# Gated cross-attention and a quantised FFN on one core: where the next tokens are normalised, and who orders VectorE

## The chip, the cores and the metric

The kernel runs on one core of one Trainium2 chip. The metric is the device time of one execution in microseconds. A core has five engines that run side by side, each with its own queue in which instructions start in order: TensorE (PE in the profile; its weight loads are shown apart as PEld), VectorE (DVE), ScalarE (ACT), GpSimd (POOL) and SyncE (SP), which here only issues DMAs. They wait for each other by semaphores.

## The reference

The shapes are x (8, 256, 1024), the context (8, 256, 1024), square attention weights of 1024, and FFN weights of 2752 x 1024 (gate, up) and 1024 x 2752 (down), all f32. Cut to what matters:

```python
def fake_quant(t, axis):                       # symmetric, 127 steps
    s = maximum(max(abs(t), axis) / 127, 1e-8)
    return clip(round(t / s), -128, 127) * s

def xattn(text, f):
    Q = text @ Wq.T + bq;  K = f @ Wk.T + bk
    return softmax(Q @ K.T / sqrt(1024)) @ f   # values are the raw context

def ffn(x):
    gate, up = qlinear(x, w_gate), qlinear(x, w_up)   # inputs and weights fake-quantised by row
    return qlinear(silu(gate) * up, w_down)

x = x + tanh(g_xattn) * xattn(layernorm(x), ctx)
x = x + tanh(g_ffn) * ffn(layernorm(x))
```

## The kernel before

**Tiles.** There are B = 8 sequences of 256 tokens; a sequence is NTT = 2 tiles of 128 tokens. The width 1024 is KC = 8 chunks of 128, or two halves of 512. The FFN width 2752 is 21 chunks of 128 and one of 64, which the code handles as NPR = 11 pairs.

**First stage, to about 108 us.** The product of the two attention weights is formed once (seven half-size products, L313), so that scores are tokens times this matrix `mt` times context.

**Attention loop (L645 to L695), b = 0 to 6, about 46 us each.** The scores of sequence b are formed in `softmax_stage`, which also transposes the already normalised tokens `xn` of b+1 on TensorE; ScalarE copies the transposes into `xT` (L436). Then the queries H of b+1 are formed in eight parts (`queries_between(0)` to `(7)`, L508, copied out by ScalarE at L512). Between these parts lie the rest of the work of sequence b and the preparation for later ones: two calls of `attend` (the "attended halves" are the two token tiles of b), `residual` (VectorE, L566), the statistics of the new tokens x2 (`Rows.sums`, `root`, `inverse`), their normalising and rounding steps (`steps`, `store_steps`), storing x2 to HBM through GpSimd's queue (L667, L674), transposing the context of b+1 (`features_transposed`), and loading and normalising the tokens xn of b+2 (L661 and L680 to L691). `prepare()` is a software pipeline over the FFN weights: SyncE loads a piece, VectorE takes its row maxima (L118) and the inverse of the step, GpSimd scales it (L209, L221), ScalarE rounds it (L245, L234), and it is transposed or stored by DMA. A piece passes these three steps in three successive calls.

From L164 to L928 `tc.manual_schedule()` holds: every engine runs its instructions in the order in which the code writes them.

**The last attention with the first FFN block (L882 to L928), about 469 to 516 us.** The pairs of the FFN's first block lie between the parts of the last sequence's attention.

**FFN (L941 to L1009).** A block is one sequence. `gate_up(block, p)` forms pair p: `products` fills a bank g and a bank tr (L749, two of each), VectorE multiplies gate by the token's step (`silu_gate`, L758), ScalarE applies Silu (L760), VectorE makes h (`hidden`, L773), ScalarE takes its absolute value (L779), and `fold` keeps a running maximum (L790). A block's down products (`down_pair`, L854) fill four banks (tags s and a) with the rounded hidden tiles `hq` of the block before; between its eleven pairs the maxima of the newer block become steps (`block_max`, `block_scales`), are spread over the partitions through two ScalarE instructions and two transposes (`broadcast_rows`, L712, L713) and are copied out as `ib` (L826), and `quantised` makes the next hq: VectorE's product (L839) and a rounding by VectorE (L841) or by two ScalarE instructions (L843, L844). `down_end` takes each of the four outputs (two token tiles, two halves) out of its bank (VectorE, L871), adds the residual xr (GpSimd, L874) and stores it (L875); `o` has three buffers, xr two.

In this part only TensorE has its order from the code:

```python
order.enter_context(tc.manual_schedule(engines={mybir.EngineType.PE}))
```

The order on VectorE, ScalarE, GpSimd and SyncE comes from a planner, which places instructions by its own estimate of when they can run.

Of the kernel before, what the change touches and what calls it, by code (L numbers as in the profile page):

```python
# [17 lines left out]
P = 128  # L18
# [9 lines left out]
def gated_xattn_ffn_kernel(  # L28
# [26 lines left out]
    nc = tc.nc  # L55
    B, S, D = x.shape
# [109 lines left out]
    if True:  # L166
# [347 lines left out]
        def features_transposed(b, g, copy):  # L514
            quarter_transposed(fT, [f_tiles[b][:, l, :] for l in range(NLT)], g, copy)

        def load_tokens(b, tag):
            tiles = []
            for t in range(NTT):
                tiles.append(work.tile([P, D], F32, name=tag, tag=tag))  # L520
                nc.sync.dma_start(out=tiles[t], in_=x[b, t * P : (t + 1) * P, :])
            return tiles
# [22 lines left out]
        def numerators_transposed(pe):  # L545
            pt = transposes(pe, range(NLT))
            pT = work.tile([P, NLT, P], F32, name="pT", tag="pT", bufs=1)
            nc.scalar.copy(pT, pt[:, :NLT, :])
            return pT
# [93 lines left out]

        waiting = None
        for b in range(B - 1):  # L645
            nums = softmax_stage(b, xn)
            tokens_bias(b + 1, xn, scratch)
            if waiting:
                store_steps(*waiting)
            queries_between(0)  # L650
            xr = load_tokens(b, "xr")
            pT = numerators_transposed(nums[0][0])
            prepare()
            queries_between(1)
            pas = attend(b, pT)
            pT = numerators_transposed(nums[1][0])
            residual(b * NTT, pas, xr[0], nums[0][1])
            prepare()
            queries_between(2)
            if b + 2 < B:  # L660
                xn = load_tokens(b + 2, "xn")  # L661
            features_transposed(b + 1, 0, nc.scalar.copy)
            pas = attend(b, pT)
            residual(b * NTT + 1, pas, xr[1], nums[1][1])
            stats = Rows()
            stats.sums(0, xr[0])
            nc.gpsimd.dma_start(out=x2_dram[b * NTT], in_=xr[0])  # L667
            prepare()
            queries_between(3)
            stats.sums(1, xr[1])  # L670
            stats.root()
            if b + 2 < B:
                load_features(b + 2, (f_right, f_left)[b % 2])
            nc.gpsimd.dma_start(out=x2_dram[b * NTT + 1], in_=xr[1])  # L674
            features_transposed(b + 1, 1, nc.scalar.copy)
            stats.inverse()
            queries_between(4)
            y = steps(b * NTT, xr[0], stats)
            features_transposed(b + 1, 2, nc.scalar.copy)
            if b + 2 < B:  # L680
                stats_n = Rows()
                for t in range(NTT):
                    stats_n.sums(t, xn[t])
            queries_between(5)
            store_steps(b * NTT, y)
            features_transposed(b + 1, 3, nc.scalar.copy)
            if b + 2 < B:
                stats_n.root()
                stats_n.inverse()
                for t in range(NTT):  # L690
                    normalise(xn[t], xn[t], stats_n, t)  # L691
            queries_between(6)
            y = steps(b * NTT + 1, xr[1], stats)
            queries_between(7)
            waiting = (b * NTT + 1, y)  # L695
# [242 lines left out]

    order.enter_context(tc.manual_schedule(engines={mybir.EngineType.PE}))  # L941
    ALL = [(t, half) for t in range(NTT) for half in range(NH)]
    for p in range(9, NPR):
        gate_up(first, p)
# [18 lines left out]
    for b in range(1, B):  # L963
        if b > 1:
            block = {"xq": xq, "sx": sx_next, "h": []}
            for p in range(NPR):
                gate_up(block, p)
        if b + 1 < B:
            xq, sx_next = load_quantised(b + 1), sx
        pds = down_start()  # L970
        next_hq = []
        for p in range(NPR):
            down_pair(pds, hq, p, ALL)
            if p == 3:
                am = block_max(block, "g")
            if p == 5:
                next_sh, ib = block_scales(b, am, "tr")
            if p == 7 and b + 2 < B:
                sx = token_steps(b + 2, "g")
            if p > 4:  # L980
                for q in range(len(next_hq), NPR if p == NPR - 1 else len(next_hq) + 2):
                    next_hq.append(quantised(block["h"][q], ib, q))
            if b == 1 and p in (1, 2, 3, 4):
                n = 2 * P
                pb = bank("tr")
                broadcast_rows(pb[:, :n], swd[:, 2 * p - 2 : 2 * p], late[0])
                nc.scalar.copy(swd_bc[:, (p - 1) * n : p * n], pb[:, :n])
        down_end(b - 1, pds, sh, ALL)
        sh, hq = next_sh, next_hq

    pds = {key: bank(tag) for key, tag in zip(ALL, ("g", "tr", "s"))}
    for key in ALL[:3]:
        for p in range(NPR):
# [50 lines left out]
```

## Time and profile before

| | |
|---|---|
| runs shown, us | 951.08, 953.9, 5640.63; median 953.9 |
| the profiled execution's own time, us | 949.75 |
| its span, first to last instruction, us | 948.0 |
| TensorE busy, us | 930.9 |
| VectorE busy, us | 640.3 |
| ScalarE busy, us | 370.0 |
| GpSimd busy, us | 151.6 |

All lines come from that one execution. A row of the order of time gives start and duration in us, engine, line, operation, out<-in with shapes, a count, and in brackets how long the engine had been idle before it and what ended that. A row of the list of waits gives who waited for whom, the sum in us, how often, and the longest. A row of the groups gives count, busy us and mean ns of one. "PE ps_g L508" is TensorE writing a bank of tag g at line 508. The parts of the attention loop begin with the first query product of a sequence, at 146.54, 192.89, 239.65, 287.87, 335.29 and 381.37 us.

### The profile page before, as it was taken

To read this page: it belongs to the slowest core of one execution; us is meant where nothing else is said; L and a number is where in the kernel's file an instruction comes from. 1 tells how busy PE (TensorE), PEld (TensorE's weight loads), DVE (VectorE), ACT (ScalarE), POOL (GpSimd) and SP (SyncE) were. 2 spreads that over 40 slices of the span, in tenths; PEclk is the share of its full clock that TensorE was granted. 3 is DMA by queue.
4 is the path that set the end of the run, shared out by engine and by line. 5 is a ranking of instruction groups with operands and counts; after the bars stand their busy time and mean duration, and the time that the engine had idled before them with its cause. 6 is when DMAs were issued, how large, how long until landed. Compare 5 with 4: busy or idle time off the path is not lost.

```text
span 948.0 us, 14269 instructions
## 1 busy us (share of the span) xinstructions
PE 930.9 (98%) x5496; PEld 692.2 (73%) x5496; DVE 640.3 (68%) x1326; ACT 370.0 (39%) x668; POOL 151.6 (16%) x160
## 2 busy tenths in 40 slices
PE   9999999999999999999999999999999999999997
PEld 5444687878687878787878867858678685876854
DVE  5976834959585868686467857675676666667673
ACT  0122434545454535454547862414324143341410
POOL 0032311121221221221100003011030110303005
PEclk9999999999999999999999999999999999999999
DMA  9256776959597887978393712012121111201004
GB/s 345 99 148 226 211 213 183 335 184 301 191 265 251 238 257 234 235 252 236 103 191 74 148 23 90 9 30 76 23 90 23 31 59 23 90 1 67 25 1 156
DMA packets 125716, 135.95 MB, mean 143 GB/s; under 512 B 90256, under 2 KB 91536, under 8 KB 125648
## 3 DMA queue, kind: packets, MB, share of 16 engines
q1 hardware_dynamic: 112368, 104.36, 40.3%
q0 software_dynamic: 4784, 16.52, 4.4%
q10 hardware_dynamic: 8496, 14.16, 4.1%
q8 instruction: 43, 0.70, 0.3%
q14 instruction: 25, 0.20, 0.1%
HBM read 87.04 MB, written 26.74 MB: 120 GB/s over the span
## 4 chain that ended last, share of the span: by engine, by line
PE 61%; DVE 17%; issue 9%; DMA 6%; ACT 4%; POOL 2%; SPq 1%; ACTq 0%; DVEq 0%; POOLq 0%
PE ps_tr L749 10%; PE ps_g L749 10%; PE ps_g L508 10%; PE ps_s L508 5%; PE ps_a L555 4%; PE ps_a L854 4%; PE ps_s L854 4%; PE ps_s L313 4%; PE ps_a L313 4%; DVE h L839 3%; PE ps_s L526 2%; PE ps_g L313 2%; DMA out_dram<-o 2%; DMA wdq_dram<-rq 2%; PE ps_tr L413 2%
## 5 line engine op out<-in xcount | busy, mean ns | idle before, releaser
L508 PE MATMUL ps_g<-xT,mt 128*128 128x256 f32 x640 | 145.2, 380 | 3.7 <-ACT xT L436 3.7
L508 PEld LDWEIGHTS ps_g<-xT,mt 128*128 128x128 f32 x640 | 119.9, 190 | 24.3 <-ACT xT L436 5.9
L760 ACT ACTIVATE g<-g,swg 128x256 f32<-128x256 f32 (+1 forms) x176 | 79.7, 500 | 147.2 <-DVE g L758 146.6
L854 PEld LDWEIGHTS <-hq 128*128 128x128 bf16 x726 | 71.1, 98 | 74.7
L773 DVE SCALAR_TENSOR_TENSOR h<-ps_tr,swu,g 128x256 f32<-128x256 f32 x168 | 74.7, 482 | 48.5 <-ACT g L760 45.1
L209 POOL TENSOR_SCALAR raw<-raw,inv 128x1024 f32<-128x1024 f32 (+1 forms) x44 | 54.6, 1242 | 256.3 <-DVE inv L114 148.4
L874 POOL TENSOR_TENSOR o<-o,xr 128x512 f32<-128x512 f32 x31 | 39.7, 1281 | 327.8 <-DVE o L871 239.4
L749 PE MATMUL ps_tr<-xqb,wuT_lo 128*128 128x256 bf16 x704 | 84.7, 273 | 2.6 <-DVE h L773 2.6
L508 PE MATMUL ps_s<-xT,mt 128*128 128x256 f32 x384 | 86.9, 379 | 0.0
L790 DVE TENSOR_TENSOR acc<-acc,g 128x512 f32<-128x512 f32 (+2 forms) x88 | 56.4, 642 | 42.0 <-ACT g L779 41.2
L749 PE MATMUL ps_g<-xqb,wgT_lo 128*128 128x256 bf16 x704 | 84.7, 273 | 0.0
L749 PE MATMUL ps_tr<-xqb,wuT_hi 128*128 128x256 bf16 x640 | 77.7, 273 | 0.2
L749 PE MATMUL ps_g<-xqb,wgT_hi 128*128 128x256 bf16 x640 | 77.7, 273 | 0.2 <-DVE g L758 0.2
L245 ACT ACTIVATE rq<-raw,nmagic 128x1024 bf16<-128x1024 f32 (+1 forms) x44 | 50.6, 1149 | 69.4 <-POOL raw L209 60.3
L508 PEld LDWEIGHTS ps_s<-xT,mt 128*128 128x128 f32 x384 | 71.2, 190 | 8.7
L749 PEld LDWEIGHTS <-wuT_lo 128*128 128x128 bf16 x704 | 68.9, 98 | 11.5 <-issue 3.6
L749 PEld LDWEIGHTS <-wgT_lo 128*128 128x128 bf16 x704 | 69.0, 98 | 9.7 <-issue 0.6
L839 DVE TENSOR_TENSOR h<-h,ib 128x512 f32<-128x512 f32 x88 | 57.0, 683 | 22.1 <-ACT ib L826 22.1
L749 PEld LDWEIGHTS <-wuT_hi 128*128 128x128 bf16 x640 | 62.6, 98 | 7.9 <-issue 0.6
L749 PEld LDWEIGHTS <-wgT_hi 128*128 128x128 bf16 x640 | 62.6, 98 | 7.6 <-issue 0.4
L779 ACT ACTIVATE g<-h 128x512 f32<-128x512 f32 (+2 forms) x88 | 51.8, 590 | 38.5 <-DVE h L773 37.7
L566 DVE SCALAR_TENSOR_TENSOR xr<-ps_a,r,xr 128x512 f32<-128x512 f32 x32 | 23.9, 751 | 62.3 <-PE ps_a L555 62.2
(177 smaller groups left out, 1375.6 us busy)
## 6 DMA issues: line engine op xcount, KB each, us to landing
raw<-in_L_ffn_w_down_dram SPq DMA_DIRECT2D x32, 512.0 KB, 6.1
raw<-in_L_ffn_w_gate_dram SPq DMA_DIRECT2D x21, 512.0 KB, 4.9
raw<-in_L_ffn_w_up_dram SPq DMA_DIRECT2D x21, 512.0 KB, 5.5
fn<-in_ctx_dram SPq DMA_DIRECT2D x8, 1024.0 KB, 6.8
xr<-in_x_dram SPq DMA_DIRECT2D x16, 512.0 KB, 4.7
x_dram<-xr POOLq DMA_DIRECT2D x16, 512.0 KB, 5.6
xr<-x_dram SPq DMA_DIRECT2D x32, 256.0 KB, 3.5
out_dram<-o POOLq DMA_DIRECT2D x31, 256.0 KB, 3.8
```

The lines of the kernel that those rows point to most:

```text
L209: nc.gpsimd.tensor_scalar(raw[:n], raw[:n], inv, MAGIC, ALU.mult, ALU.add)
L245: nc.scalar.activation(rq[:n], raw[:n], AF.Identity, bias=nmagic[:n])
L313: nc.tensor.matmul(pm, lhsT=a[:, c, k * P : (k + 1) * P], rhs=b[:, c, :], start=start, stop=stop)
L508: nc.tensor.matmul(ph, lhsT=mt[:, k, j * P : (j + 1) * P], rhs=xT[:, k, :], start=(k == 0), stop=(k == KC - 1),)
L749: nc.tensor.matmul(pb[:, i, :], lhsT=w[:, k, :], rhs=block["xq"][:, k, :], start=(k == 0), stop=(k == KC - 1),)
L760: nc.scalar.activation(g[:n, i, :], g[:n, i, :], AF.Silu, scale=swg[:n, c : c + 1])
L773: nc.vector.scalar_tensor_tensor(h[:n, i, :], src, swu[:n, c : c + 1], g[:n, i, :], ALU.mult, ALU.mult)
L779: nc.scalar.activation((block["acc"] if p == 0 else g)[:n, i, :], h[:n, i, :], AF.Abs)
L790: nc.vector.tensor_tensor(acc[:n, i, :], acc[:n, i, :], g[:n, i, :], ALU.max)
L839: nc.vector.tensor_tensor(h, h, ib.to_broadcast((P, 2, TB)), ALU.mult)
L854: nc.tensor.matmul(pds[t, half][:, cols], lhsT=hq[p][:, i, t * P : (t + 1) * P], rhs=wd[:, half * HB + cols.start : half * HB + cols.stop] ...
L874: nc.gpsimd.tensor_tensor(o, o, xr, ALU.add)
```

## The change

Four things are altered.

In the attention loop the tokens of b+2 are loaded right after those of b (before, after the third query part), their statistics are taken between the two attended halves, and they are normalised ahead of the second one. The two stores of x2 follow their residuals directly. `stats.inverse()` of x2 is written behind `queries_between(4)`.

In the FFN VectorE, too, gets the order that the code writes.

The four outputs of a block no longer leave their banks together: one does so at once, and each of the other three after one of the first three pairs of the next block (after the loop, one behind the other).

From the second block on, the tiles hq of even number are rounded by ScalarE instead of VectorE. At b = 1 the broadcasts of the down weights' steps go from pairs 1, 2, 3, 4 to pairs 2, 4, 6, 8.

```diff
@@ the attention loop @@
         for b in range(B - 1):
+            nxt = b + 2 < B
...
             xr = load_tokens(b, "xr")
+            if nxt:
+                xn = load_tokens(b + 2, "xn")
             pT = numerators_transposed(nums[0][0])
             prepare()
             queries_between(1)
             pas = attend(b, pT)
             pT = numerators_transposed(nums[1][0])
             residual(b * NTT, pas, xr[0], nums[0][1])
+            nc.gpsimd.dma_start(out=x2_dram[b * NTT], in_=xr[0])
+            if nxt:
+                stats = Rows()
+                for t in range(NTT):
+                    stats.sums(t, xn[t])
+                stats.root()
             prepare()
             queries_between(2)
-            if b + 2 < B:
-                xn = load_tokens(b + 2, "xn")
+            if nxt:
+                stats.inverse()
+                for t in range(NTT):
+                    normalise(xn[t], xn[t], stats, t)
             features_transposed(b + 1, 0, nc.scalar.copy)
             pas = attend(b, pT)
             residual(b * NTT + 1, pas, xr[1], nums[1][1])
+            nc.gpsimd.dma_start(out=x2_dram[b * NTT + 1], in_=xr[1])
             stats = Rows()
             stats.sums(0, xr[0])
-            nc.gpsimd.dma_start(out=x2_dram[b * NTT], in_=xr[0])
             prepare()
             queries_between(3)
             stats.sums(1, xr[1])
             stats.root()
-            if b + 2 < B:
+            if nxt:
                 load_features(b + 2, (f_right, f_left)[b % 2])
-            nc.gpsimd.dma_start(out=x2_dram[b * NTT + 1], in_=xr[1])
             features_transposed(b + 1, 1, nc.scalar.copy)
+            queries_between(4)
             stats.inverse()
-            queries_between(4)
             y = steps(b * NTT, xr[0], stats)
             features_transposed(b + 1, 2, nc.scalar.copy)
-            if b + 2 < B:
-                stats_n = Rows()
-                for t in range(NTT):
-                    stats_n.sums(t, xn[t])
             queries_between(5)
             store_steps(b * NTT, y)
             features_transposed(b + 1, 3, nc.scalar.copy)
-            if b + 2 < B:
-                stats_n.root()
-                stats_n.inverse()
-                for t in range(NTT):
-                    normalise(xn[t], xn[t], stats_n, t)
             queries_between(6)
@@ the FFN @@
-    order.enter_context(tc.manual_schedule(engines={mybir.EngineType.PE}))
+    order.enter_context(
+        tc.manual_schedule(engines={mybir.EngineType.PE, mybir.EngineType.DVE})
+    )
...
             for p in range(NPR):
                 gate_up(block, p)
+                if ends:
+                    down_end(*ends.pop(0))
...
-                    next_hq.append(quantised(block["h"][q], ib, q))
-            if b == 1 and p in (1, 2, 3, 4):
+                    next_hq.append(
+                        quantised(block["h"][q], ib, q, nc.scalar if q % 2 == 0 else nc.vector)
+                    )
+            if b == 1 and p in (2, 4, 6, 8):
                 n = 2 * P
                 pb = bank("tr")
-                broadcast_rows(pb[:, :n], swd[:, 2 * p - 2 : 2 * p], late[0])
-                nc.scalar.copy(swd_bc[:, (p - 1) * n : p * n], pb[:, :n])
-        down_end(b - 1, pds, sh, ALL)
+                broadcast_rows(pb[:, :n], swd[:, p - 2 : p], late[0])
+                nc.scalar.copy(swd_bc[:, (p - 2) * P : p * P], pb[:, :n])
+
+        ends = [(b - 1, pds, sh, [key]) for key in ALL]
+        down_end(*ends.pop(0))
         sh, hq = next_sh, next_hq
 
+    for end in ends:
+        down_end(*end)
     pds = {key: bank(tag) for key, tag in zip(ALL, ("g", "tr", "s"))}
```

## The prediction

> **What bounds the kernel now.** I read the page first (shares and granted clock), then the list of waits for TensorE alone, then the order of time around each of those waits.
>
> ```profile
> PE 930.9 (98%) x5496; PEld 692.2 (73%) x5496; DVE 640.3 (68%) x1326; ACT 370.0 (39%) x668; POOL 151.6 (16%) x160
> ...
> PEclk9999999999999999999999999999999999999999
> ```
>
> TensorE works 930.9 of 948.0 us at full clock. [...] So what can be won is TensorE's idle time, 17.1 us with start and tail. Its longest waits:
>
> ```profile
> PE ps_g L508 <- ACT xT L436: 3.7, 5, 1.1
> PE ps_tr L413 <- ACT xT L436: 2.8, 2, 2.1
> PE ps_tr L749 <- DVE h L773: 2.6, 5, 1.3
> ```
>
> One of the 3.7 (0.24) is ahead of the loop, so 6.2 us lie in the attention loop and 2.6 in the FFN. Where the first come from (order of time, iteration from 239.65 to 287.87):
>
> ```profile
> 250.51 0.75 DVE L566 SCALAR_TENSOR_TENSOR xr<-ps_a,r,xr 128x512 f32<-128x512 f32 x1 [0.96 <-PE ps_a L555]
> 251.18 1.21 DVE L118 TENSOR_REDUCE wam<-raw 128x1 f32<-128x1024 f32 x1
> ...
> 256.40 0.75 DVE L566 SCALAR_TENSOR_TENSOR xr<-ps_a,r,xr 128x512 f32<-128x512 f32 x1 [3.25 <-PE ps_a L555]
> ```
> ```profile
> 283.36 1.15 ACT L245 ACTIVATE rq<-raw,nmagic 128x1024 bf16<-128x1024 f32 x1 [3.75 <-POOL raw L209]
> 284.41 1.05 ACT L436 COPY xT<-ps_tr 128x512 f32<-128x512 f32 x2
> ...
> 285.03 1.14 PE L413 MATMUL ps_tr<-ident,xn 128*128 128x128 f32 x8 [2.07 <-ACT xT L436]
> ...
> 285.81 0.42 DVE L534 TENSOR_REDUCE nm<-ps_s 128x1 f32<-128x256 f32 x1
> ...
> 286.78 0.47 ACT L542 ACTIVATE pe<-ps_s,nm 128x256 f32<-128x256 f32 x1
> ```
>
> VectorE idles between the two attended halves and is late at the end: the first scores are complete at 280.2, VectorE takes their maximum at 285.81. ScalarE's queue holds a weight rounding (fed by GpSimd, fed by VectorE's inverse) and the exponential ahead of the xT copies, so VectorE's lateness becomes TensorE's wait. And in the FFN:
>
> ```profile
> 637.04 0.74 DVE L871 SCALAR_TENSOR_TENSOR o<-ps_a,sh,swd_bc 128x512 f32<-128x512 f32 x1
> ...
> 638.41 0.91 ACT L760 ACTIVATE g<-g,swg 128x256 f32<-128x256 f32 x2 [9.55 <-DVE g L758]
> ...
> 642.46 0.75 DVE L871 SCALAR_TENSOR_TENSOR o<-ps_a,sh,swd_bc 128x512 f32<-128x512 f32 x1 [3.02 <-DMA out_dram<-o]
> ...
> 643.13 0.48 DVE L773 SCALAR_TENSOR_TENSOR h<-ps_tr,swu,g 128x256 f32<-128x256 f32 x1
> ...
> 643.66 1.91 PE L749 MATMUL ps_tr<-xqb,wuT_lo 128*128 128x256 bf16 x16 [1.29 <-DVE h L773]
> ```
>
> The fourth output waits 3.02 us for a free o, half of an h stands behind it on VectorE, and with it a bank.
>
> **Attention part, walked on this iteration.** Moved on VectorE: xn's sums (272.10 to 275.15, 3.05), inverse (0.95 undisturbed, as at 266.44) and two normalises (1.54). New order from residual(0)'s end at 251.26: sums 254.3, weight maximum (1.58) 255.9, inverse 256.8, normalises 258.4, residual(1) (1.7) 260.1, against 258.8 before. Then 6.1 of sums and weight steps as at 258.7 to 264.85: 266.2. The root follows at once, since xn's root has loaded the table (1.28, one load per iteration as before, now beside VectorE's sums). So fT's second copy ends at 266.9, as before; its bank is due at 269.10. On: weight step 267.7, inverse 268.6, steps(0) (3.2) 271.8, two weight steps 275.0, steps(1) 278.2, down-weight maximum 279.4: ahead of the scores' end at 280.2, 5.5 us earlier than before. Exponential then near 283.6, last xT copies 284.9, due 285.4. The wait is gone with 0.9 + 0.5 us to spare; next late are these last copies.
>
> Queues passed. SP: xn's two loads go ahead of up to three raw loads; they wait for tokens_bias (291.15 in the next iteration), which ends before the second xr load gets its buffer (292.43), so nothing new blocks. Raws land up to 2.6 us later (512 KB landed every 1.3 us there); VectorE's waits for raws were 2.1 us in the whole run, so 0, or +1 at worst. GpSimd: x2's stores pass two weight scalings, which now stand behind residual(0) (from 293.0 to about 300); their roundings stand behind H's third copy, near 302.5 there, so 0, at worst +1. ScalarE: xn's root holds a rounding, H's third copy and fT's first copy until 254.6; that last bank is due at 265.2: free.
>
> [...] Rows: a 2-element VectorE step took 0.99 for 0.34 beside a scaling (277.08), a product 1.75 for 1.22 (240.79): 0.5 to 0.65 each. [...] I take the rows and leave 0.7 of 6.2: **-5.5**, bounds -6.2 and +1.
>
> **FFN part.**
>
> ```profile
> L841 DVE TENSOR_SCALAR hq<-h 128x512 bf16<-128x512 f32 x77 | 29.2, 417 | 0.0
> ...
> L844 ACT ACTIVATE hq<-h,nmagic 128x512 bf16<-128x512 f32 x11 | 7.7, 712 | 0.0
> ...
> L843 ACT ACTIVATE h<-h,magic 128x512 f32<-128x512 f32 x11 | 7.4, 712 | 0.2 <-DVE h L839 0.2
> ```
>
> Per block VectorE loses six roundings (6 x 0.42 = 2.5), ScalarE gets 6 x 1.42 = 8.5, beside its idle 9.55 and without a table load (L843 and L844 ran between the Silus with none). From ib at 625.4, eleven products at 0.6 apart and five roundings end at 634.3; ScalarE needs 1.42 per 1.65 us of VectorE's, so it keeps up. First output at 635.0, g at 635.9, h by 637.5, due at 642. Each further output (0.74) goes behind a pair: 2.33 + 0.74 = 3.07 of TensorE's 3.49; with 3.49 between them o's are free (add and issue 2.14, landing 3.8). With sums of pair p-1 before h of p, no wait for Abs remains. **-2.6**; bounds -2.6 and, if ScalarE's list puts the last rounding ahead of each block's Silu and h comes 1.4 late, still -2.6: the slack is over 4.
>
> First and second block (516 to 556): the fixed order holds g(2) behind the first product, which waits for ib (528.4): g(2) ends 529.7, h(2) 531.9, its bank is due 533.1. After that a pair is product 0.6, rounding 1.42, Silu 0.91 and h 0.54 later, about 3.5 in all, against 3.49; two broadcasts at pair 5 put 1.05 on ScalarE. The slack of 1.2 is nearly used: **+0.3**, bounds -0.2 (today's broadcast wait) and, with ScalarE's order against it at 4.0 a pair, +3.5.
>
> Down phase of b = 1: swd's broadcasts move from pairs 1 to 4, where ScalarE was free, to 2, 4, 6, 8. Between those of 6 and 8 lie 3.9 us of TensorE; ScalarE has cb and copies (2.1) and two or three roundings (2.8 to 4.3) there: 4.9 to 6.4, so 1.0 to 2.5 of wait. Bounds 0 (every cb ahead of the roundings) and 4.3 (three roundings ahead of a cb); I take **+1.5**, once.
>
> Tail: outputs are paced by o, xr and GpSimd. The last xr landed at 943.6 and is the late one; its chain starts with o at 924.36, now about 923.0 (914.37 + 11 x 0.6 + 5 x 0.41): **-1.3**, bounds -2.3 (TensorE's end 941.6 then decides) and 0.
>
> **Sum.** -5.5 - 2.6 + 0.3 + 1.5 - 1.3 = -7.6. Against the profiled execution's own 949.75 (span 948.0) that is 942.2. The runs shown, 951.08 and the median 953.9, lie 1.3 and 4.2 above it; half-way of what the three show is +1.8: **944.0**.
>
> **Rivals.** (1) The wait changes hands: the waits were ScalarE's for GpSimd's chain and half of them stay (the 3.75 row speaks for it; against it that the chain starts at VectorE, now early): -7.6 + 3.1, about 947 on the median's footing. (2) ScalarE's list, still free, collides in both FFN places at their upper bounds: +3.2 + 2.8, near 950. For it: ScalarE is then in every pair's loop. (3) Slower: xn lands late and all of VectorE stands behind its sums.
>
> ```profile
> DMA to landing us min/median/max: 4.6/6.2/9.7
> ```
>
> The second xn is issued 0.9 after the second xr's issue (292.43, say), its sums come up 8.75 after that: 7.9 us are covered, 1.4 more is spare, and at 10.3 the old waits are back. The six loads took 5.4 to 9.65; the worst fills only part of the spare. At 12 us each, 1.7 x 6 = +10, with the rest -2.1: 960. Against it: the late ones stood behind three raws, which they now precede. 2% slower needs 14 us.
>
> **Chances.** Forecast 0.52 (940 to 947), (1) 0.17, (2) 0.17, (3) 0.08, collisions that I have not named 0.06, half of them dear. About 2%, 19 us, is what a measurement of this kernel can tell from no change; the idle time cannot give that (930.9 busy, 1.1 before, 4 after): faster 0.02. Slower: part of (3) and of the unnamed, 0.06. The range, 939 to 957, takes in (1), (2) and the near half of (3).
>
> **What would show it.** Waits of TensorE for xT under 1 us and for h none; the maximum nm right behind the scores; VectorE's 3.25 us between the halves filled by sums of xn with no DMA before them; VectorE's wait for out_dram gone outside the tail; L841 x35; TensorE waiting for cb at b = 1 about 1.5. Wrong it would be by sums of xn behind a DMA wait, by h or g behind roundings of ScalarE, or by TensorE waiting for fT.

## The result

The changed kernel takes 937.07 us (median; 936.7 to 937.68), beside 951.19 us for the kernel before on the same chip. The ratio is 0.9849, 95% interval 0.983 to 0.9867: 14 us faster, 6.9 us under the forecast's 944.0 and 1.9 us below its range. (One of the five runs of before is the 5640.63 us shown above; the ratio leaves it out.) The profiled execution took 936.96 us with a span of 935.2 us.

The page of the changed kernel, the rows that answer to those shown of before:

```profile
PE 927.7 (99%) x5496; PEld 692.0 (74%) x5496; DVE 634.8 (68%) x1284; ACT 430.3 (46%) x752; POOL 148.0 (16%) x160
```

The same 5496 matmuls now show 3.2 us less busy time, though 930.9 had been taken as the floor. That will matter below. The list of waits for TensorE (who waited for whom, sum in us, times, longest), complete:

```profile
PE ps_tr L337 <- DVE magic L87: 1.1, 1, 1.1
PE ps_g L313 <- DVE mt L352: 0.7, 1, 0.7
PE ps_g L508 <- ACT xT L436: 0.2, 1, 0.2
PE ps_tr L413 <- ACT fT L436: 0.2, 1, 0.2
PE ps_g L750 <- DVE g L759: 0.2, 1, 0.2
```

The waits for xT in the loop and those for h are gone; what is left is the start, one wait in the first stage (L313, outside the change) and three of 0.2, of which the one for xT is ahead of the loop.

To see where the 12.76 us of span went, I measured stages from the first matmul of one group to the first matmul of another, in both traces (us). By this measure the loop of before begins at 146.38; the 146.54 given above counts from the end of the preceding matmul's record.

| stage | before | after | difference | forecast |
|---|---|---|---|---|
| start to the second sequence's queries | 146.38 | 146.76 | +0.38 | 0 |
| attention loop, to the scores of b = 7 | 317.14 | 309.21 | -7.93 | -5.5 |
| last scores to the first FFN block | 7.57 | 7.56 | 0 | 0 |
| first and second FFN block | 84.47 | 84.26 | -0.21 | +0.3 |
| down phase of b = 1 | 20.52 | 20.68 | +0.16 | +1.5 |
| blocks b = 2 to 7, to the last down phase | 326.89 | 323.34 | -3.55 | -2.6 |
| last down phase, to TensorE's end | 38.64 | 38.64 | 0 | 0 |
| TensorE's end to the span's end | 6.34 | 4.73 | -1.61 | -1.3 |

Every term that the forecast named came out at its value or better; the +0.38 is in the first stage, which the change doesn't touch. In the loop an iteration before took 46.51, 46.76, 48.22, 47.42, 46.08 and 45.46 us; after, 45.78 and then 45.35 each time. A block of the FFN takes 57.20 us every time, start to start; before, 57.33 to 58.65. (The last interval reads 56.98: there is no sequence b+2 left at b = 6, so two transposes of 0.11 us each fall away, in both kernels.) The repetitions have become equal, and the list shows no wait in them but one of 0.2 in the first iteration.

The order of time of the iteration from 237.89 (the one before began at 239.65), VectorE and ScalarE, shows the new place of the work:

```profile
248.65 0.75 DVE L566 SCALAR_TENSOR_TENSOR xr<-ps_a,r,xr 128x512 f32<-128x512 f32 x1 [0.96 <-PE ps_a L555]
249.32 1.27 DVE L132 BATCH_NORM_STATS2 st<-xn 128x6 f32<-128x512 f32 x2
...
257.61 1.41 DVE L566 SCALAR_TENSOR_TENSOR xr<-ps_a,r,xr 128x512 f32<-128x512 f32 x2
...
278.67 1.07 ACT L436 COPY xT<-ps_tr 128x512 f32<-128x512 f32 x2 [0.95 <-PE ps_tr L413]
279.03 0.41 DVE L534 TENSOR_REDUCE nm<-ps_s 128x1 f32<-128x256 f32 x1
```

The sums of xn start as the first attended half leaves its bank, with no DMA ahead of them; the second half comes up with no idle time before it, where VectorE idled 3.25 us before the change. The maximum nm follows 41.14 us into the iteration; before it was 46.16. So VectorE is 5.0 us earlier at the end, where the forecast had 5.6, and the xT copies now wait for TensorE, not TensorE for them. In the FFN one output stands between two pairs:

```profile
626.75 0.74 DVE L872 SCALAR_TENSOR_TENSOR o<-ps_s,sh,swd_bc 128x512 f32<-128x512 f32 x1
627.63 0.69 DVE L759 TENSOR_TENSOR g<-ps_g,sx 128x512 f32<-128x512 f32 x1
628.35 0.91 ACT L761 ACTIVATE g<-g,swg 128x256 f32<-128x256 f32 x2
629.44 0.88 DVE L774 SCALAR_TENSOR_TENSOR h<-ps_tr,swu,g 128x256 f32<-128x256 f32 x2 [1.13 <-PE ps_tr L750]
```

g follows o at once, and h waits for TensorE's products, no longer behind an output that waits for a free o. The other signs that the prediction named are there too: VectorE rounds 35 tiles (L842 in this kernel), and its waits for out_dram, 23.1 us before, are 9.7 and all behind the last block's products. One sign is absent: the wait of about 1.5 for cb at b = 1.

### The profile page after: what moved, and what is told of

Read it like the earlier page. It is cut to its first block, busy times and chain, and to the rows that moved or that the text cites. A ratio compares the mean times of both kernels' runs of the same rounds, so it can differ in the third digit from the quotient of the medians.

```text
span 935.2 us, 14303 instructions
## 1 busy us (share of the span) xinstructions
PE 927.7 (99%) x5496; PEld 692.0 (74%) x5496; DVE 634.8 (68%) x1284; ACT 430.3 (46%) x752; POOL 148.0 (16%) x160
## 4 chain that ended last, share of the span: by engine, by line
PE 84%; issue 6%; DMA 4%; DVE 4%; ACT 2%; POOL 1%; SPq 0%; ACTq 0%; DVEq 0%; POOLq 0%
PE ps_g L508 14%; PE ps_g L750 14%; PE ps_tr L750 13%; PE ps_s L508 8%; PE ps_a L855 6%; PE ps_s L855 6%; PE ps_s L526 6%; PE ps_a L555 6%; PE ps_tr L413 3%; PE ps_s L313 3%; PE ps_a L313 3%; DMA A<-in_L_xattn_Wq_dram 2%; DMA xr<-x_dram 1%; DVE h L774 1%; PE ps_g L313 1%
## 5 line engine op out<-in xcount | busy, mean ns | idle before, releaser
L759 DVE TENSOR_TENSOR g<-ps_g,sx 128x512 f32<-128x512 f32 x88 | 60.7, 689 | 40.8 <-PE ps_g L750 37.7
L791 DVE TENSOR_TENSOR acc<-acc,g 128x512 f32<-128x512 f32 (+2 forms) x88 | 61.7, 702 | 1.8 <-ACT g L780 0.8
```

The source lines that it names most:

```text
L759: nc.vector.tensor_tensor(g, pg, block["sx"].to_broadcast((P, 2, TB)), ALU.mult)
L791: nc.vector.tensor_tensor(acc[:n, i, :], acc[:n, i, :], g[:n, i, :], ALU.max)
```

## The experiments

Two theories at the start. **A**: the parts act apart, each where the forecast put it (the loop through VectorE's earlier work, the blocks through the outputs that no longer hold VectorE), and only their sizes were misread. **B**: something that the forecast had at nothing carries a part of the gain: the stores' places, the fixed order by itself, ScalarE's roundings. The batches ran beside the kernel before, at 950.56, 950.58 and 951.73 us in the order of the runs below. Stage lengths are measured as above; "FFN rest" runs from the start of block b = 2 to TensorE's end (365.53 before, 361.98 after), since a missing matmul record in some traces shifts the border within it by 0.2. They come from one traced execution of each kernel, and the executions of a kernel differ: those of `spread_only` have spans of 935.6, 936.8, 937.6 and 937.6 us, and the traced one is the shortest.

| kernel | median us | ratio, interval | loop | down b=1 | FFN rest | tail |
|---|---|---|---|---|---|---|
| before | - | - | 317.14 | 20.52 | 365.53 | 6.34 |
| after | 937.07 | 0.9849, 0.983-0.9867 | 309.21 | 20.68 | 361.98 | 4.73 |
| attn_only | 941.17 | 0.9897, 0.9865-0.993 | 309.22 | 20.52 | 364.97 | 5.02 |
| ffn_only | 945.71 | 0.9947, 0.9928-0.9965 | 319.45 | 20.68 | 361.98 | 3.92 |
| norm_late | 944.39 | 0.9932, 0.991-0.9954 | 317.53 | 20.68 | 361.99 | 4.49 |
| xn_twice | 963.62 | 1.013, 1.0097-1.0163 | 334.37 | 20.68 | 361.98 | 4.71 |
| stores_old | 939.7 | 0.9864, 0.9839-0.989 | 313.00 | 20.68 | 361.98 | 4.74 |
| ends_together | 944.9 | 0.9936, 0.9915-0.9958 | 309.22 | 20.68 | 370.03 | 4.34 |
| dve_free | 939.1 | 0.9874, 0.9847-0.9902 | 309.23 | 23.13 | 361.99 | 4.02 |
| no_act_round | 940.1 | 0.9885, 0.9864-0.9906 | 309.22 | 20.52 | 361.99 | 7.41 |
| all_act_round | 948.12 | 0.9959, 0.9942-0.9975 | 309.21 | 29.42 | 365.84 | 4.02 |
| swd_early | 942.46 | 0.9909, 0.9889-0.9928 | 309.22 | 25.84 | 361.99 | 5.48 |
| spread_only | 939.34 | 0.9859, 0.9833-0.9886 | 309.21 | 20.52 | 361.98 | 5.86 |
| tail_bufs | 935.6 | 0.9828, 0.9802-0.9854 | 309.21 | 20.68 | 361.98 | 3.97 |

### Each part alone

The changed loop with the FFN of before (`attn_only`):

```diff
-    order.enter_context(
-        tc.manual_schedule(engines={mybir.EngineType.PE, mybir.EngineType.DVE})
-    )
+    order.enter_context(tc.manual_schedule(engines={mybir.EngineType.PE}))
...
-                if ends:
-                    down_end(*ends.pop(0))
...
+                    next_hq.append(quantised(block["h"][q], ib, q))
-            if b == 1 and p in (2, 4, 6, 8):
+            if b == 1 and p in (1, 2, 3, 4):
...
+        down_end(b - 1, pds, sh, ALL)
```

> The new attention loop with the old FFN. Theory A (a wait of TensorE costs its recorded idle and 0.16 us more, and short waits are not recorded at all, so the cost is read from start to start): the seven parts take 45.4 us each, 7.9 less in all, nothing in the FFN: span about 940.0, time 943.3. Rival B (the recorded idle is the whole cost, and the rest of the 12.8 us lies elsewhere): 6.2 less, 945.0.

The loop of before with the changed FFN (`ffn_only`):

```diff
-            if nxt:
-                xn = load_tokens(b + 2, "xn")
...
-                    stats.sums(t, xn[t])
-                stats.root()
...
             queries_between(5)
...
+                stats_n.root()
+                stats_n.inverse()
+                for t in range(NTT):
+                    normalise(xn[t], xn[t], stats_n, t)
```

> The old attention loop with the new FFN. A: the blocks lose 3.55 (2.6 recorded), the tail 1.6, the rest nothing: 5.2 less, span 942.8, time 946.0, and with attn_only the parts add up to the whole change. B: 2.6 and 1.3 less, 947.3, and the parts do not add up.

The loop part gives -9.4 us, the FFN part -4.9, together -14.2 against -14.1 for the whole. That the sums agree so well is in part luck: `attn_only` has a tail 1.3 us shorter than before with the same code there, and the loop of `ffn_only` takes 2.3 us longer than before, 1.7 of it a stretch at half clock (told at the end). That the parts act apart is shown by the stages: loop and blocks have the lengths of the changed kernel where their part is in, to 0.01 us, and the old kind of waits where it is not (for h 2.0 us in `attn_only`, for xT 7.5 in `ffn_only`).

### The loop: which of the moves pays

`norm_late` keeps the new places of the loads and stores, and puts the statistics and the normalising of xn back behind the scores' start:

```diff
-            if nxt:
-                stats = Rows()
-                for t in range(NTT):
-                    stats.sums(t, xn[t])
-                stats.root()
...
+            if nxt:
+                stats_n = Rows()
+                for t in range(NTT):
+                    stats_n.sums(t, xn[t])
...
+                stats_n.root()
+                stats_n.inverse()
```

> The new kernel, but xn's statistics and normalising stand at the end of the loop's body again; its load and x2's stores stay early. If moving VectorE's work is what paid: VectorE comes late to the maxima again, the waits for xT return, 6 to 8 us: about 944. If the earlier load or the stores paid: 937.

The loop is back at 317.53 us, 8.3 over the changed one (1.7 of it a stretch at half clock, told at the end). TensorE's waits in `norm_late`:

```profile
PE ps_g L508 <- ACT xT L436: 3.5, 5, 1.1
PE ps_tr L413 <- ACT xT L436: 2.2, 2, 2.0
```

These are the waits of before with little taken off (3.7 and 2.8 there). So what pays is that VectorE's work is moved; loads and stores at their new places bring little or nothing without it.

`stores_old` asks whether the places of the two x2 stores matter once that work has moved:

```diff
-            nc.gpsimd.dma_start(out=x2_dram[b * NTT], in_=xr[0])
-            if nxt:
...
             stats.sums(0, xr[0])
+            nc.gpsimd.dma_start(out=x2_dram[b * NTT], in_=xr[0])
...
+            nc.gpsimd.dma_start(out=x2_dram[b * NTT + 1], in_=xr[1])
             features_transposed(b + 1, 1, nc.scalar.copy)
```

> The changed kernel with x2's two stores at their old places (after the statistics and the scalings). First theory (the place of the stores is worth nothing, VectorE's order is what pays in the loop): the loop stays at 309.2 us, the total within 0.5 us of 937.0. Rival (the stores set when xr comes free for the next loads, or hold GpSimd's scalings): waits for fT or xT return, the loop grows by 1 us or more.

Here the rival was right. The loop grows by 3.8 us in this trace; the median is 2.6 above the changed kernel's, with intervals that overlap, so this rests on the trace. SyncE's order of time in the iteration from 145.82, transposing DMAs and loads (`stores_old`):

```profile
166.37 3.18 SPq L246 DMA_TRANSPOSE wgT_lo<-rq  x1
169.65 0.83 SPq L194 DMA_DIRECT2D raw<-in_L_ffn_w_down_dram  x1
...
177.78 3.75 SPq L246 DMA_TRANSPOSE wgT_lo<-rq  x1
181.62 0.53 SPq L194 DMA_DIRECT2D raw<-in_L_ffn_w_down_dram  x1
```

and in the changed kernel, 0.94 us later in its frame:

```profile
167.33 1.32 SPq L246 DMA_TRANSPOSE wgT_lo<-rq  x1
168.74 0.72 SPq L194 DMA_DIRECT2D raw<-in_L_ffn_w_down_dram  x1
...
177.86 1.35 SPq L246 DMA_TRANSPOSE wgT_lo<-rq  x1
179.31 0.53 SPq L194 DMA_DIRECT2D raw<-in_L_ffn_w_down_dram  x1
```

With the old places the first store is issued at 164.73 and lands at 172.31; SyncE's transpose at 166.37 falls into it and holds SyncE 3.18 us instead of 1.32. (At the new places it runs from 158.59 to 161.67, ahead of these transposes.) The second store (174.35 to 179.89) runs beside the context load and the transpose at 177.78. A store in flight is not enough by itself: in the changed kernel the transpose at 175.00 falls into the second store (169.84 to 176.69) and holds SyncE 1.23 us. What goes with the long ones is the number of transfers in flight, SyncE's own and x2's stores together. Counted over the loop of all 14 traces, a transpose that starts with at most three of them in flight held SyncE more than 1.8 us in 17 of 380 cases, with four or more in 69 of 80. In the two rows above the store is the fourth; in the changed kernel there are three. The raw loads behind them are issued late, and VectorE, which runs here in the order written, waits 2.82 us for one (`stores_old`, order of time):

```profile
185.32 1.22 DVE L118 TENSOR_REDUCE dam<-raw 128x1 f32<-128x1024 f32 x1 [2.82 <-DMA raw<-in_L_ffn_w_down_dram]
```

Then nm stands at 191.05, in the changed kernel at 189.16 (2.8 us of delay, by the 0.94 between the frames), and TensorE waits 1.65 us for xT at 193.54. The chain from the late raw to TensorE is in the trace. That the store, as the fourth transfer, lengthens the transposes is inferred from this count; no run varies the number in flight alone.

`xn_twice` tests the forecast's slower rival, in which xn lands late and all of VectorE stands behind its sums. Each load of xn is done twice, and the sums need the second:

```diff
                 xn = load_tokens(b + 2, "xn")
+                for t in range(NTT):
+                    nc.sync.dma_start(out=xn[t], in_=x[b + 2, t * P : (t + 1) * P, :])
```

> The new kernel with each load of xn done twice, one behind the other, so that the tokens land about 5 us later and VectorE's sums wait for them. By the walk the tightest part has 1.4 us to spare and others up to 3.5: a delay of about 4.5 us gives 1 to 3 us of wait in each of six parts, 943 to 955, with VectorE waiting for the DMA of xn. If the landing does not matter at this size: 937.

It is 1.3% slower than before: 26.5 us over the changed kernel, and dearer than had been expected. The groups and the waits of `xn_twice`:

```profile
L132 DVE BATCH_NORM_STATS2 st<-xn 128x6 f32<-128x512 f32 x28 | 17.9, 682 | 29.7 <-DMA xn<-in_x_dram 29.7
```
```profile
PE ps_tr L413 <- ACT fT L436: 19.5, 6, 5.0
```

VectorE waits 29.7 us for xn, and TensorE 19.5 us for fT, in six waits. The cause of the second in the order of time (`xn_twice`, ScalarE):

```profile
225.07 1.15 ACT L245 ACTIVATE rq<-raw,nmagic 128x1024 bf16<-128x1024 f32 x1 [3.34 <-POOL raw L209]
226.93 0.20 ACT L138 ACTIVATE rt<-v 128x2 f32<-128x2 f32 x1 [0.71 <-DVE v L135]
227.03 0.57 ACT L436 COPY fT<-ps_tr 128x512 f32<-128x512 f32 x1
```

The copies of fT stand behind a weight rounding and the root on ScalarE, which wait for VectorE (v, and the inverse that GpSimd scales with), which was late by its wait for xn. TensorE waited 3.45 us for this copy. The rival's mechanism is real, but its place is fT and not the xT of old. Of the 25.2 us that the loop grew by, some 4.8 are three stretches at half clock behind these waits (an estimate: half of the 9.6 us of work in them). Part of the rest may be the doubled loads' own traffic, which this run can't set apart. What keeps it away in the changed kernel is the landing time: the list of DMAs of xn gives

```profile
DMA to landing us min/median/max: 3.6/5.9/7.0
```

against the 7.9 us that the forecast had found to be covered.

### The FFN: which of the moves pays

`ends_together` keeps VectorE in the written order and lets the four outputs leave their banks at once:

```diff
-                if ends:
-                    down_end(*ends.pop(0))
...
-        down_end(*ends.pop(0))
+        for end in ends:
+            down_end(*end)
```

> The new kernel with VectorE's order fixed, but all four outputs of a block leave together as before. By the walk: the fourth output waits for the first one's store (about 6 us after it), the next block's first g stands behind it, and TensorE waits about 1.8 + 0.16 for its bank at the third pair of six blocks: 937 + 12 = 949. If the slack of a block covers it: 937.

The FFN rest grows by 8.1 us, to 4.5 more than before the change. VectorE, `ends_together`:

```profile
629.18 0.74 DVE L872 SCALAR_TENSOR_TENSOR o<-ps_a,sh,swd_bc 128x512 f32<-128x512 f32 x1
633.99 0.75 DVE L872 SCALAR_TENSOR_TENSOR o<-ps_a,sh,swd_bc 128x512 f32<-128x512 f32 x1 [4.07 <-PE ps_tr L750]
634.66 0.68 DVE L759 TENSOR_TENSOR g<-ps_g,sx 128x512 f32<-128x512 f32 x1
```

The fourth output came 4.07 us late and the block's first g stood behind it; TensorE waited 0.59 to 1.45 us for that g in each of six blocks. (The bracket names TensorE's products, which this output doesn't read. It waited for the free o: the store of the block's first output landed at 633.87, 0.12 us before it.) In the kernel before, the planner had put g ahead of the fourth output, as the prediction's rows show. A fixed order without the spread would have been a loss.

`dve_free` keeps the spread and ScalarE's roundings and gives VectorE's order back to the planner:

```diff
-        tc.manual_schedule(engines={mybir.EngineType.PE, mybir.EngineType.DVE})
+        tc.manual_schedule(engines={mybir.EngineType.PE})
```

> The new kernel, but VectorE's order in the FFN from the planner again; outputs stay spread over pairs, ScalarE rounds every other pair. If the spread of the outputs removed the wait for h: about 937.5, no wait of TensorE for h. If the fixed order did it: the 3.55 us come back, 940.6.

`no_act_round` keeps the fixed order and lets VectorE round all tiles from the second block on:

```diff
-                        quantised(block["h"][q], ib, q, nc.scalar if q % 2 == 0 else nc.vector)
+                        quantised(block["h"][q], ib, q)
```

> The new kernel with all roundings from the second block on by VectorE. It adds 6 x 0.42 = 2.5 us to VectorE at each block's end; by the walk g and h are then 2.5 later with more than 4 us of slack, so no wait of TensorE: 937, the tail up to 1.3 longer. If ScalarE's share is what removed the waits for h: up to 3.6 us come back, 940.5.

`spread_only` has both edits, and swd's broadcasts at their old pairs, so that of the FFN's changes the spread alone is left:

```diff
-            if b == 1 and p in (2, 4, 6, 8):
+            if b == 1 and p in (1, 2, 3, 4):
```

> The changed kernel with the attention loop as changed, but in the FFN one edit alone: the outputs leave their banks one behind each pair. VectorE's order is the planner's again, VectorE rounds all, and swd's broadcasts are at pairs 1 to 4. First theory (a wait for h comes from an output that holds VectorE while it waits for a free o, so spreading the outputs is enough): blocks b = 2 to 7 at 323.5 us against 326.5 with the old FFN, the b = 1 down phase at 20.5, the tail at 5 to 7, total 937.5 to 939 us. Rival (the fixed order or ScalarE's share is needed as well): the blocks stay near 326.5, total about 940.5 us.

All three have the FFN rest of the changed kernel, 361.98 or 361.99 us, and no wait for h or g beyond 0.2. So the whole gain in the blocks b = 2 to 7 comes from one edit, the spread of the outputs; the fixed order and ScalarE's share are worth nothing there. (The fixed order is worth the 0.2 in the first and second block: 84.26 to 84.33 us in all runs that have it, 84.42 to 84.47 in those that leave VectorE to the planner.) In `no_act_round` the tail is 2.7 us longer: behind the last block's products and roundings the outputs of b = 6 begin to leave their banks at 915.69 instead of 912.36, with TensorE's end only 0.3 later. `spread_only` has a span of 935.6 us, almost that of the changed kernel; its tail is 1.1 longer (outputs from 912.51; what makes the 1.1 was not traced).

`dve_free` has one stage that is worse, the down phase of b = 1, by 2.45 us:

```profile
PE ps_g L714 <- ACT cb L713: 1.0, 1, 1.0
...
PE ps_tr L714 <- ACT cb L713: 0.9, 2, 0.6
```

That is the collision of swd's broadcasts with the roundings on ScalarE, which the forecast had priced at +1.5 for the changed kernel. It comes here, with the planner ordering VectorE, and not with the fixed order. `swd_early` is the changed kernel with the broadcasts at their old pairs, the edit shown last:

> The new kernel with the down weights' steps broadcast at pairs 1 to 4 again. The forecast priced the later place at +1.5 us, the trace shows 0.16 more in that phase: by the trace 937.0 and no change that can be told, by the forecast 935.5.

The down phase of b = 1 takes 5.2 us more than in the changed kernel, with one wait of 3.2 us:

```profile
PE ps_tr L714 <- ACT cb L713: 3.2, 1, 3.2
```

On ScalarE two roundings of hq (553.72 to 556.19: two additions, 1.33 together, and two steps of 1.32 together) stand ahead of the broadcasts of pair 2, for which TensorE waits from 553.7 to 556.9. That is 3.4 of the 5.2 us; behind it lies a stretch at half clock, which is worth some 1.7. So the broadcasts' move is not a price of the change but something that the changed FFN needs: with the planner's order and VectorE's roundings (`spread_only`) the old pairs cost nothing, 20.52 us. Whether the fixed order alone asks for the move, or only together with ScalarE's roundings, was not run.

`all_act_round` gives ScalarE all eleven roundings:

```diff
-                        quantised(block["h"][q], ib, q, nc.scalar if q % 2 == 0 else nc.vector)
+                        quantised(block["h"][q], ib, q, nc.scalar)
```

> The changed kernel, with all eleven roundings of a block's h on ScalarE instead of six of them. First theory (what pays in the FFN is VectorE's freedom and the spread outputs, and ScalarE has room up to a point): eleven roundings of 1.42 to 1.45 us are 16 us and start some 7.6 us before the next block, so they end about 8.4 us into it; the block's first Silu stands behind the last of them, h(0) comes about 1.1 us after its bank is due at 8.7 us, and a wait of about 1.3 us returns in each of six blocks: the blocks grow from 323.5 to 331, the total to about 945 us. Rival (ScalarE's list puts the Silus ahead of the last roundings): no wait, 323.5 and about 937 us.

The time, 948.12 us, is near what the first theory said, but not for its reason: the blocks have no wait at all. ScalarE in the block from 633.56 (`all_act_round`):

```profile
638.75 0.71 ACT L844 ACTIVATE h<-h,magic 128x512 f32<-128x512 f32 x1
639.37 0.50 ACT L761 ACTIVATE g<-g,swg 128x256 f32<-128x256 f32 x1
639.77 0.71 ACT L845 ACTIVATE hq<-h,nmagic 128x512 bf16<-128x512 f32 x1
```

The eleven took 14.25 us from 626.23 (two tiles taken together cost 1.23 each, not 1.42), and half of a Silu was let in before the last step. The loss is where ScalarE has other duties or no cover: 8.7 us in the down phase of b = 1 (waits for cb of 3.3 and 2.8), and 3.9 in the last down phase, where TensorE comes for the last hq (0.9 and 0.8). Each of the two has a stretch at half clock in it, worth some 1.7 us. Nothing between six and eleven was tried.

### The tail

`tail_bufs` is the changed kernel with the last sequence's outputs and residuals in buffers of h, free by then, and the last residual loaded earlier:

```diff
-            o = late[0].tile([P, HB], F32, name="o", tag="o", bufs=3)
+            o = (
+                early.tile([P, HB], F32, name="o", tag="h", bufs=HBUFS)
+                if b == B - 1 else late[0].tile([P, HB], F32, name="o", tag="o", bufs=3)
+            )
...
+    t, half = ALL[3]
+    xr = load_residual(B - 1, t, half)
```

> The changed kernel, but the last sequence's outputs and residuals take buffers of h, which are free by then, and the last residual is loaded ahead of the third output's end. First theory (the tail is set by the last add, which waits 1.3 us for xr and, ahead of it, 1.65 us for a free o): the tail shrinks from 4.7 to 3.7-4.1 us, total about 936.2 us. Rival (what sets the end is the last matmul and the landing of the last store, about 3 us): nothing changes, 937.0 us.

VectorE's end in the changed kernel:

```profile
928.79 0.48 DVE L1016 SCALAR_TENSOR_TENSOR o<-ps_a,sh,swd_bc 128x256 f32<-128x256 f32 x1 [1.65 <-DMA out_dram<-o]
930.60 0.42 DVE L1019 TENSOR_TENSOR o<-o,xr 128x256 f32<-128x256 f32 x1 [1.32 <-DMA xr<-x_dram]
```

and in `tail_bufs`:

```profile
929.90 0.48 DVE L1022 SCALAR_TENSOR_TENSOR o<-ps_a,sh,swd_bc 128x256 f32<-128x256 f32 x1 [1.39 <-PE ps_a L855]
930.42 0.42 DVE L1025 TENSOR_TENSOR o<-o,xr 128x256 f32<-128x256 f32 x1
```

The output now waits for TensorE alone, and the last add for nothing: that is shown. The tail is 3.97 us, 0.76 shorter, and 935.6 us is the lowest median, at 0.9828 of before, but that the buffers brought this is not shown. The intervals overlap, and `ffn_only`, whose FFN is that of the changed kernel word for word, has a tail of 3.92. What remains is the way from TensorE's end (929.86) through VectorE to the landing of the last store (932.67), 2.8 us, and 1.2 after it. The tails of the other kernels lie between 3.9 and 7.4 us; their differences were not traced to a cause beyond what is told above.

## Why the prediction was wrong

The places and the chains of the waits that the change removes were right; the sizes were not. The step that failed is **"So what can be won is TensorE's idle time"**, with 930.9 us of busy time as what remains. It capped the loop at 6.2 us and the blocks at 2.6, and they gave 7.93 and 3.55: 2.9 of the 6.9 us by which 944.0 was off, the largest single part. In these traces recorded idle time is less than what a wait costs. The records of neighbouring matmuls overlap (by 0.16 us in the rows below), so the comparison goes by starts. The order of time of before around one wait of the loop, TensorE only, shows it:

```profile
236.62 1.89 PE L526 MATMUL ps_s<-fT,H 128*128 128x256 f32 x8
239.65 3.72 PE L508 MATMUL ps_g<-xT,mt 128*128 128x256 f32 x16 [1.14 <-ACT xT L436]
243.20 0.38 PE L413 MATMUL ps_tr<-ident,pe 128*128 128x128 f32 x2
243.42 3.62 PE L508 MATMUL ps_g<-xT,mt 128*128 128x256 f32 x16
```

Undisturbed, the group of 8 takes 1.73 us from its first start to the next group's first (8 x 0.216), but its row lasts 1.89: the last matmul's record runs 0.16 us into the next one's time. So the next start was due at 238.35 and came at 239.65, 1.30 us late, where the bracket shows 1.14. And the 16 matmuls after the wait need 3.72 us where the next 16 need 3.62: 0.10 more, between the first two. In these traces a wait costs its recorded idle time + 0.16, and in the loop up to 0.10 more, and one shorter than 0.16 shows no idle time at all. By starts the same profile gives 16 such matmuls 3.45 us to the next group's first where there was no wait (272.99 to 276.44) and 3.55 just after this one (239.65 to 243.20); the forecast drew nothing from the 0.10.

Because TensorE's order is the same in both kernels, the loop can be compared matmul by matmul, start to start. Of the 7.93 us that it lost, 5.99 were recorded idle time; 0.82 more lay at those same starts, and 1.11 at starts with little or no recorded idle time (0.10 behind a wait six times, late starts of 0.20 and 0.13 with 0.04 and 0 recorded, and small ones). In the blocks: 3.55 = 2.56 recorded + 0.82 at the same five starts + 0.17. The shrinking busy time is the same thing from the other side: TensorE's busy time holds a 0.16 tail for each wait, and the 0.10 after it.

By the forecast's own steps, profiled time against profiled time:

- **Attention, -5.5**: -7.93. Its walk holds: nm comes right behind the scores, the sums fill the idle stretch, the xT copies no longer make TensorE wait. Of the difference of 2.4, 1.9 are the waits' unrecorded part, and 0.5 is the 0.7 reserve, of which 0.2 was needed (the wait of 0.2 for fT in the first iteration).
- **"x2's stores ... so 0, at worst +1"**: the places were costed as the price of the new ones, and there was none. What was not seen is that the old ones would have cost 3.8 us of loop, through transposes that held SyncE 3.18 and 3.75 us where the changed kernel shows 1.32 and 1.35 (put down above to the store as the fourth transfer in flight, which is inferred), and so through VectorE's next raw.
- **The 0.7 left of the 6.2**: no run shows this term. The changed loop takes 45.35 us in five of six iterations, and the one wait in it is 0.2. Of the rows that it was weighed with, one was misread: the step at 277.08 takes 0.16 us undisturbed, not the 0.34 set against its 0.99, which is the mean over all its 16 runs, the disturbed ones with them:

```profile
266.84 0.16 DVE L146 TENSOR_TENSOR rz<-rz,rt 128x2 f32<-128x2 f32 x1
...
276.95 1.12 POOL L209 TENSOR_SCALAR raw<-raw,inv 128x1024 f32<-128x1024 f32 x1 [6.28 <-DVE rr L143]
277.08 0.99 DVE L146 TENSOR_TENSOR rz<-rz,rt 128x2 f32<-128x2 f32 x1
```

It ends at 278.07, with the scaling. In all 14 traces this step started 94 times beside a GpSimd instruction that had more than 0.17 us to go, and each time it ended within 0.013 us of that one's end. Row maxima and sums keep their length beside a scaling (medians in both kernels: 1.20 to 1.21 and 0.68 us beside one, 1.21 and 0.68 away from it). So in these traces a moved scaling costs this step what is left of the scaling when the step comes up, and does not hold whatever VectorE does for its whole length.
- **TensorE's busy time, 930.9**: taken as what remains, it is no floor, since the same 5496 matmuls show 927.7 after the change. Weight loads are busy for 74% of that span, and TensorE has no wait left in the loop and the blocks but two of 0.2.
- **FFN, -2.6**: -3.55, again by the waits' unrecorded part. The sum credited the spread, ScalarE's roundings and the fixed order together; the spread alone gives all of it.
- **First and second block, +0.3**: -0.21, at its lower bound. The wait for the broadcast is gone, and the fixed order is what removed it.
- **Broadcasts at b = 1, +1.5**: +0.16, near the lower bound. The sum put each cb behind two or three whole roundings. ScalarE's list lets a cb in between the two halves of a rounding, and so a cb waits for half a rounding, 0.71 us. The order of time of ScalarE in the changed kernel:

```profile
562.63 0.71 ACT L844 ACTIVATE h<-h,magic 128x512 f32<-128x512 f32 x1
563.25 0.39 ACT L713 ACTIVATE cb<-ones,swd 128x128 f32<-128x128 f32 x1
563.54 0.71 ACT L845 ACTIVATE hq<-h,nmagic 128x512 bf16<-128x512 f32 x1
```

- **Tail, -1.3**: -1.61, inside its bounds, but in part by luck. Against TensorE's end its outputs begin 0.85 us earlier than before (912.36 to 930.46, before 924.36 to 941.61), where 1.36 had been summed, and the tails of the four other kernels with this FFN unchanged go from 3.92 to 4.74.
- **Footing, +1.8**: here the five runs lie 0.1 above the profiled execution (936.96), and the kernel before 1.4 above its own. That is 1.7 of the 6.9 us by which 944.0 was off; the sum, -7.6 against -12.8, is the other 5.2: 2.4 loop, 1.0 blocks, 0.5 first blocks, 1.3 broadcasts, 0.3 tail, less the 0.4 of the first stage, which the change doesn't touch. Of the 5.2, 2.9 are the failed step (1.9 in the loop, 1.0 in the blocks); the rest are terms set too cautiously.

The rivals: (1) no half of the waits stayed. (2) ScalarE's list did not collide under the order chosen; with the broadcasts at their old pairs or all roundings on ScalarE it does, by 5.2 and 12.6 us (half clock included), where the rival gave 6.0 for both places. (3) is real, at about twice its price (in the iteration of `xn_twice` from which the rows are, the second xn landed 11.6 us after its first issue, for which its sum gives some 13 us over the forecast; it was 26.5 over the changed kernel), and was kept away by loads of 3.6 to 7.0 us. The chance of "within 2%" (0.92) was rightly high: the ratio is 0.985.

## What to carry to other kernels

Read what a stage could win from its length, start to start, against its own undisturbed repetition (45.35 us a turn, 57.20 a block), and not from the sum of idle times, which here left out 0.16 to 0.27 us for each wait and the short waits whole. An engine with an ordered queue that is late at the end of a turn and idle in the middle should do the work for the next turn in the middle, if the data is there by then with room to spare: the same move won 8 us in the loop with loads of 6 us and lost 17 with loads doubled. Where several outputs leave banks together and wait for buffers, let one leave between two pieces of other work before anything else is tuned.

## What the runs showed of the hardware

In some of the traces TensorE runs at half its clock for some 3.4 us behind a wait. The order of time in `norm_late`, behind a wait of 2.01 us:

```profile
280.27 1.89 PE L526 MATMUL ps_s<-fT,H 128*128 128x256 f32 x8
284.18 1.14 PE L413 MATMUL ps_tr<-ident,xn 128*128 128x128 f32 x8 [2.01 <-ACT xT L436]
285.16 3.47 PE L526 MATMUL ps_s<-fT,H 128*128 128x256 f32 x8
```

and its granted clock there (columns: window, length, busy time of PE, PEld, DVE, ACT, POOL, the clock as a share of full speed, DMA share, GB/s):

```profile
286.00:287.00 1.00, 1.00 (x4) 0.82 (x3) 0.94 (x1) 1.00 (x4) 0.00 (x0) 0.50 1.51 93
```

Eight matmuls take 3.47 us where eight of the same shape took 1.89 some 5 us earlier. Over all traces eight such stretches were found inside the kernels (by matmuls that follow each other at 0.427 us instead of 0.216). By the granted clock the one in `norm_late` lasts 3.4 us: its means over the four us from 285 are 0.65, 0.50, 0.50 and 0.64, which makes 3.4 us at 0.50. The one in `ffn_only` reads 0.50 from 286 to 289 and 0.97 over the seven us behind that, 3.4 again. Full of work, one costs half of that, 1.7 us (an estimate from the 3.4). Seven stood behind a wait of 2 us or more; the eighth, at the end of `all_act_round`, behind two of 0.9 and 0.8. Several waits of 2 to 3.5 us had none behind them, among them the 2.07 of the kernel before, where the granted clock reads 1.00 in every us from 285 to 289. So a wait of 2 us cost here 2 us or, by the estimate, nearly 4, and its length does not tell which: 2.0 us, and once 0.9 and 0.8, had a stretch behind them, and 3.5 once had none.
